# Causal attention: another order of the query blocks, two merged band steps, and other engines at the attentions' ends

## The chip, the cores and the metric

The kernel runs on one core of a Trainium2 chip. The metric is the device time of one execution, in microseconds (us), given as a median of several. Engines are named as in the profile: PE is TensorE's matrix multiplication (PEld its weight loads), DVE is VectorE, ACT is ScalarE, POOL is GpSimd and SP is SyncE, which here issues DMAs. Everything is computed in 32-bit floating point.

## The reference

The program is a block of two layers on an input of 2 sequences of 2048 tokens with 256 features. Every sublayer normalizes its input first and adds its result to it:

```python
x = x + 0.5 * _L0_ffn_ref(_layernorm(x), ...)   # mixture of 6 experts, two for each token
x = x + _L0_attn_ref(_layernorm(x), ...)        # full softmax attention, 16 heads of 16
x = x + 0.5 * _L0_ffn_ref(_layernorm(x), ...)
x = x + 0.5 * _L1_ffn_ref(_layernorm(x), ...)   # a gated recurrence over the 2 sequences
x = x + _L1_attn_ref(_layernorm(x), ...)        # causal attention
x = x + 0.5 * _L1_ffn_ref(_layernorm(x), ...)
```

The change is mostly in the causal attention:

```python
q = _apply_rotary_interleave(q, cos, sin); k = _apply_rotary_interleave(k, cos, sin)
q = q / sqrt(DIM_PER_HEAD)
scores = jnp.einsum('bhqd,bhkd->bhqk', q, k)
rel_idx = jnp.clip(pos[None, :] - pos[:, None], -32, 32) + 32
rel = rel_emb[rel_idx]
scores = scores + jnp.einsum('bhqd,qkd->bhqk', q, rel)
scores = jnp.where(causal[None, None], scores, NEG_INF)
attn = jax.nn.softmax(scores, axis=-1)
ctx = jnp.einsum('bhqk,bhkd->bhqd', attn, v)
ctx = ctx + jnp.einsum('bhqk,qkd->bhqd', attn, rel)
out = ctx.transpose(0, 2, 1, 3).reshape(B, L, MODEL_DIM) @ w_o.T
```

A key more than 32 places behind its query gets the same relative term as all such keys. So only a band of keys near each query needs a term of its own.

## The kernel before, in words

**Order.** Each engine runs its instructions in the order in which the program emits them; nothing reorders them. Loops over numbered steps write that order. A step's own work is found in tables, and other work ("jobs" and "sends") is put down for a step by number.

**Tiles.** A sequence has 4 blocks of 512 tokens; a block has four chunks of 128. The 16 heads form 4 groups of 4 heads (`J`). A unit of attention is a *group*: (sequence b, query block qc, head group g), 64 of them in the full attention and 32 in the causal one. For a group the kernel does two passes over the scores. The first finds each query's maximum: PE multiplies 128 queries by up to 512 keys for one head, and DVE reduces the product to a column of maxima. The second computes scores again with keys on the partitions, with the maximum subtracted, ACT takes exponentials, and PE multiplies by the values. An additional column of ones in the values gives the softmax's sum.

**attention1 (lines 1008 to 1420), the causal attention.** `groups` lists the 32 groups in the order of work. For a group of block qc the maxima pass has 4 qc + 3 *pieces* (`pieces`): first qc times four far pieces (one chunk of queries by a block of keys, L1149 with the reduction L1158), then three band pieces (chunks 0 and 1 together, chunk 2, chunk 3). A band is 160 keys wide for 128 queries. It is first loaded with the relative terms (`by_position` makes them, ACT writes them to DRAM, `band_load` on SP reads them back skewed), DVE adds scores and takes maxima in one instruction (L1179), then reduces all maxima of a chunk to their negative, `mneg` (L1192), and one step later POOL adds that to the chunk's band (L552, 128x640). The exponentials pass has as many pieces (`key_blocks`), one or two blocks of 128 keys each: PE transposes band pieces (L1260, L1266), multiplies the rest (L1250, L1243), and ACT takes exponentials, four 128x512 or 128x384 in a piece (L1274). The step after, `weighted` multiplies by the values (L1283).

**Steps.** The lists `Ms`, `Me`, `Es`, `Ee` give each group's first and last step of the two passes. A step does one exponentials piece and one maxima piece if it has both (a *paired* step), or only the one kind. A group's exponentials come after its maxima, and a group's band tile is one of three, so its maxima wait for an earlier group's exponentials. With the order of groups that is used before, there are 319 steps, of which 257 are paired, 31 look only for maxima and 31 take only exponentials. The first steps, below zero, are preparation alone.

**Jobs.** `queries`, `keys` and `vals` prepare a pair of groups or a block: PE multiplies by weights, ACT copies, DVE shuffles, and `rotate` does the rotary rotation with three 128x512 operations, on DVE at the negative steps (L1050 is the last of them) and on POOL at the others, one, two and three steps later (`later`, by way of the helper's line L552). `queries_out` and `keys_out` have ACT put rows of heads in place (L141). `subtract` brings maxima into the queries; `positions_load`, `positions_exp`, `positions_T` and `positions` turn the stored band into the sum over relative values; `divide` transposes a group's sum (L668) and divides (L671, L672); `outputs_T` and `outputs` multiply by the output weights (L682, L691) and add to x (L697). `ln_stats` and `ln_transpose` prepare the next block's normalization.

**gather (L651).** The result of every `weighted` and `positions` is in PSUM. ACT copies it (L654), and a step later POOL adds the copy to the group's sum (L552). Both attentions use it.

**The end.** After the causal attention the last sublayer, a recurrence over 8 blocks (number = 4 x sequence + block), begins. attention1's `tail` holds statistics, normalization and transposition of the blocks 0 and 4 (`n5.stats`, `n5.normal`, `n5.turn`), done under the last exponentials. `recurrence` normalizes the others itself (L99 to L127), and skips what is there. It calls `turn(0, 0)`, then `gate(0, ...)`, `normal(0, 1)` and, inside its loop, `turn(0, 1)`, where (0, 1) is block 4.

The profile's L-numbers are of this program:

Of the kernel before, what the change touches and what calls it, by code (L numbers as in the profile page):

```python
# [17 lines left out]
P = 128  # L18
# [14 lines left out]
G = 4  # L33
# [9 lines left out]
def macaron_kernel(ctx: ExitStack, tc: tile.TileContext, t: dict, out: bass.AP):  # L43
# [510 lines left out]
    class Pieces:  # L554
# [15 lines left out]
        def later(self, units, fn, *args):  # L570

            self.due.at(self.unit + units, fn, *args)
# [78 lines left out]
        def gather(self, t, pv, parts, q0=0):  # L651

            part = self.wk.tile([P, TB], F32, name="part", bufs=parts + 2)
            nc.scalar.copy(part[:, q0:], pv[:, q0:])  # L654
            if t not in self.o:
                self.o[t] = part
                return
            o = self.o[t][:, q0:]
            self.later(1, nc.gpsimd.tensor_tensor, o, o, part[:, q0:], ALU.add)
# [57 lines left out]
    def attention0(norm, tail, rest, wq, wk_, wv, wo, bff):  # L717
# [7 lines left out]
        with ExitStack() as s:  # L725
# [61 lines left out]
            def weighted(t, kb):  # L787
                b, qc, g = groups[t]
                pv = bank()
                for j in range(J):  # L790
                    h = (g % 2) * J + j
                    nc.tensor.matmul(  # L792
                        pv[rows(j), :], lhsT=v[b, g // 2][:, kb, ds(h * VW, 32)],
                        rhs=z.pTs.pop((t, kb, j)), start=True, stop=True,
                    )
                z.gather(t, pv, 4)
# [211 lines left out]
    def attention1(norm, tail, w, relk, relv, kbias, dramp, skew):  # L1008
# [4 lines left out]
        with ExitStack() as s:  # L1013
# [3 lines left out]
            for b in range(B):  # L1017
                groups += [(b, 1, g) for g in range(G)]
                for g in range(0, G, 2):
                    groups += [(b, qc, g + i) for qc in (2, 0) for i in range(2)]  # L1020
                groups += [(b, 3, g) for g in range(G)]
# [16 lines left out]
            def rotate(xa, wa, b, qc, g):  # L1038
# [8 lines left out]
                if z.unit < 0:  # L1047
                    nc.vector.tensor_tensor(xa, xa, cos[b, qc], ALU.mult)
                    nc.vector.tensor_tensor(xb, xb, sin[b, qc], ALU.mult)
                    nc.vector.tensor_tensor(xa, xa, xb, ALU.add)  # L1050
                else:
                    op = nc.gpsimd.tensor_tensor
                    z.later(1, op, xa, xa, cos[b, qc], ALU.mult)
                    z.later(2, op, xb, xb, sin[b, qc], ALU.mult)
                    z.later(3, op, xa, xa, xb, ALU.add)
# [3 lines left out]
            def keys(b, qc, g, own):  # L1059
# [9 lines left out]
                rotate(packed[b, qc, g], w["k"], b, qc, g)  # L1069
# [22 lines left out]
            def queries(t):  # L1092
# [5 lines left out]
                rotate(q[t + 1], w["q"], b, qc, g)  # L1098
# [45 lines left out]
            def largest(t, qbs, c, j):  # L1144
# [30 lines left out]
                for qb in qbs:  # L1175
# [12 lines left out]
                    done[t, qb] = done.get((t, qb), 0) + 1  # L1188
                    if done[t, qb] < J:
                        continue  # L1190
                    mneg = z.mnegs[t % 2][:, qb]
                    nc.vector.tensor_reduce(  # L1192
                        mneg[:, :, z.row(t)], mx[t][:, qb, :, 0 : qc + 1 + (qb > 0)], AX.X,
                        ALU.max, negate=True,
                    )
                    z.later(
                        1, nc.gpsimd.tensor_tensor, band[t][:, qb], band[t][:, qb],
                        mneg[:, :, ds(z.row(t), 1)].to_broadcast([P, J, BW]), ALU.add,
                    )
# [76 lines left out]
            def weighted(t, kbs):  # L1276
# [12 lines left out]
                z.gather(t, pv, 3, max(0, kbs[0] - qc * CPB) * P)  # L1289
# [70 lines left out]
            for b in range(B):  # L1360
                for qc in range(SB):
                    f = Ms[index[b, max(qc, 1), 0]]

                    done_ = {2: 1, 3: 0}.get(qc)
# [13 lines left out]
                    for half in range(2):  # L1378
                        due = Es[index[b, max(qc, 1), 2 * half]] - 2 + 2 * (qc == 0)
                        at(due if b or qc > 1 or half else -4, vals, b, qc, half)  # L1380
# [98 lines left out]
    with tc.manual_schedule(engines=ENGINES):  # L1479
# [71 lines left out]
        tail = []  # L1551
        for i, b in enumerate((0, SB)):
            tail += [(3 + 2 * i, n5.stats, b), (4 + 2 * i, n5.normal, b, nc.vector),
                     (5 + 2 * i, n5.turn, b)]
# [96 lines left out]
```

## Time and profile before

| | |
|---|---|
| median of 5 runs | 4017.53 us (4013.49 to 4020.42) |
| profiled execution: time, span | 4018.74 us, 4017.0 us |
| granted TensorE clock, mean | 0.994 |
| PE busy | 3969.3 us (99%), 29,024 instructions |
| DVE busy | 2699.1 us (67%), 6131 |
| ACT busy | 2555.0 us (64%), 5067 |
| POOL busy | 1620.5 us (40%), 1421 |
| causal attention, first score matmul of its first paired step to that of its last step | 2605.3 to 3820.9 us |
| last recurrence's first matmul | 3835.4 us |

The profiled execution is 1.2 us over the median. Its span is the recorded part; 1.7 us lie around it. In a line of groups or of a timeline, `L1192` is the source line, `out<-in` names tiles, then come shapes and counts, busy time and the mean of one in ns, and the idle time of that engine just before, with what ended it. "PE busy" is a modelled time: matmuls are pipelined, and PE counts as busy while it runs at another engine's pace, so a stretch is judged by looking at which engine is full beside it.

### The profile page before, as it was taken

The page shows a single profiled execution, that of the slowest core. Times are in us where ns is not written, and L with a number is a line of the kernel's source. Part 1 is how long each engine was busy: PE and PEld are TensorE (multiplying, and loading weights), DVE is VectorE, ACT ScalarE, POOL GpSimd, SP SyncE. Part 2 cuts the span into 40 slices and gives each one's busy share as a digit, 9 for nine tenths or more (in the row PEclk, how much of TensorE's full clock was granted, in tenths as well). Part 3 has the DMA queues.
Part 4 walks back from the last instruction along what each step waited for, and adds up shares of the span by engine and source line. Part 5 has one row for each costly group of instructions (what it writes and reads, how often), then busy time and mean ns, then how long its engine had stood idle before and what let it go on. Part 6 is the DMA issues. An engine that isn't in the chain of part 4 may idle for free.

```text
span 4017.0 us, 78045 instructions
## 1 busy us (share of the span) xinstructions
PE 3969.3 (99%) x29024; PEld 1957.9 (49%) x29024; DVE 2699.1 (67%) x6131; ACT 2555.0 (64%) x5067; POOL 1620.5 (40%) x1421
## 2 busy tenths in 40 slices
PE   8999999999999999999999999999999999999999
PEld 5665333333344333333345655555555555555445
DVE  6247888888877788888743344667777756667634
ACT  2333888888887888888853332366657776666832
POOL 5245333337333333333444331245536655453510
PEclk9999999999999999999999999999999999999999
DMA  7341000100000000000023420254442334543201
GB/s 267 119 129 56 1 1 1 48 1 2 1 1 1 1 1 1 1 1 2 10 95 129 130 82 11 57 102 99 98 95 56 86 74 93 111 83 64 68 1 42
DMA packets 355515, 223.28 MB, mean 56 GB/s; under 512 B 146625, under 2 KB 338497, under 8 KB 355137
## 3 DMA queue, kind: packets, MB, share of 16 engines
q1 hardware_dynamic: 276800, 176.33, 17.3%
q0 software_dynamic: 12288, 33.57, 2.6%
q10 hardware_dynamic: 66048, 8.39, 1.5%
q8 instruction: 231, 3.78, 0.4%
q14 instruction: 148, 1.20, 0.1%
HBM read 113.12 MB, written 105.12 MB: 54 GB/s over the span
## 4 chain that ended last, share of the span: by engine, by line
PE 92%; DVE 4%; ACT 2%; POOL 1%; issue 1%; DMA 0%; ACTq 0%; SPq 0%; DVEq 0%; POOLq 0%
PE s L780 14%; PE s L792 13%; PE s L766 11%; PE s L148 7%; PE s L1149 7%; PE s L1283 7%; PE s L394 6%; PE s L1250 6%; PE s L414 3%; PE s L157 2%; PE s L1260 2%; PE s L691 2%; PE s L1243 1%; PE s L1266 1%; PE s L614 1%; PE s L949 1%
## 5 line engine op out<-in xcount | busy, mean ns | idle before, releaser
L552 POOL TENSOR_TENSOR part<-part 128x512 f32<-128x512 f32 (+2 forms) x768 | 950.1, 1238 | 1394.6 <-ACT part L654 1390.6
L770 DVE TENSOR_REDUCE mx<-s 128x1 f32<-128x512 f32 x2048 | 1270.5, 682 | 295.5 <-PE s L766 295.1
L785 ACT ACTIVATE pT<-s 128x512 f32<-128x512 f32 x2048 | 1063.5, 617 | 199.0 <-PE s L766 195.5
L766 PE MATMUL s<-kT,q 32*128 32x512 f32 x4096 | 1027.6, 618 | 0.2 <-DVE mx L770 0.2
L780 PE MATMUL s<-q,kT 32*128 32x512 f32 x4096 | 1018.3, 616 | 1.0 <-DVE q L649 1.0
L1274 ACT ACTIVATE pT<-s 128x512 f32<-128x512 f32 (+1 forms) x1152 | 580.6, 584 | 207.7 <-PE s L1250 102.9
L780 PEld LDWEIGHTS s<-q,kT 32*128 32x128 f32 x4096 | 417.5, 184 | 460.2 <-DVE mx L770 376.5
L654 ACT COPY part<-s 128x512 f32<-128x512 f32 (+2 forms) x832 | 500.3, 602 | 164.2 <-PE s L792 57.7
L1158 DVE TENSOR_REDUCE mx<-s 128x1 f32<-128x512 f32 (+1 forms) x768 | 472.3, 678 | 154.3 <-PE s L1149 148.7
L792 PE MATMUL s<-pT,v 128*32 128x512 f32 x4096 | 549.2, 604 | 0.7 <-ACT pT L785 0.2
L766 PEld LDWEIGHTS s<-kT,q 32*128 32x128 f32 x4096 | 410.5, 184 | 136.6 <-ACT pT L785 78.3
L1149 PE MATMUL s<-kT,q 32*128 32x160 f32 (+6 forms) x2240 | 341.5, 429 | 0.0
L1283 PE MATMUL s<-pT,v 128*32 128x512 f32 (+3 forms) x2560 | 297.3, 539 | 5.0 <-ACT pT L1274 4.8
L394 PE MATMUL s<-we,xT 128*128 x592 | 278.7, 593 | 0.2 <-ACT xT L389 0.2
L1149 PE MATMUL s<-b,q 32*128 32x512 f32 (+7 forms) x1280 | 258.8, 512 | 1.9 <-DVE mx L1158 1.9
L792 PEld LDWEIGHTS s<-pT,v 128*32 128x32 f32 x4096 | 84.4, 108 | 351.0 <-ACT pT L785 327.6
L401 DVE TENSOR_TENSOR h<-sg,s 128x256 f32<-128x256 f32 x148 | 62.3, 421 | 286.2 <-ACT sg L399 286.2
L1250 PE MATMUL s<-q,kT 32*128 32x512 f32 (+3 forms) x1152 | 242.2, 508 | 0.0
L552 POOL TENSOR_TENSOR band<-band,mneg 128x640 f32<-128x640 f32 x128 | 160.1, 1262 | 155.6 <-DVE mneg L1192 86.1
L447 POOL DMA_INDIRECT yg<-results,at x128 | 124.7, 974 | 237.8 <-DMA results<-y 198.4
L1179 DVE CUSTOM_DVE_ANT_0 band<-s,band 128x160 f32<-128x160 f32 (+1 forms) x512 | 153.6, 314 | 96.2 <-PE s L1149 61.1
L1250 PE MATMUL s<-q,b 32*128 32x512 f32 (+3 forms) x896 | 212.0, 567 | 0.0
(227 smaller groups left out, 5158.7 us busy)
## 6 DMA issues: line engine op xcount, KB each, us to landing
band<-skew SPq DMA_DIRECT2D x32, 1280.0 KB, 6.3
pd<-band SPq DMA_DIRECT2D x32, 1280.0 KB, 9.3
xs<-places SPq DMA_DIRECT2D x148, 128.0 KB, 2.2
results<-y SPq DMA_DIRECT2D x148, 128.0 KB, 1.7
places<-zero SPq DMA_DIRECT2D x2, 4736.0 KB, 23.7
we<-in_we SPq DMA_DIRECT2D x12, 768.0 KB, 9.9
skew<-s ACTq DMA_DIRECT2D x32, 256.0 KB, 3.0
s<-pd SPq DMA_DIRECT2D x32, 256.0 KB, 4.5
```

Source lines behind the costliest of these rows:

```text
L394: nc.tensor.matmul(pu, lhsT=xT[n][:, ts(kc, P)], rhs=w[:, kc, ds(val[n], 2 * D)], start=kc == 0, stop=kc == 1,)
L552: fn(*args)
L654: nc.scalar.copy(part[:, q0:], pv[:, q0:])
L766: nc.tensor.matmul(ps, lhsT=q[t][rows(j), ts(qb, P)], rhs=kT[b, g][rows(j), ts(kc, TB)], start=True, stop=True,)
L770: nc.vector.tensor_reduce(mx[t][:, qb * J + j, kc : kc + 1], ps, AX.X, ALU.max)
L780: nc.tensor.matmul(st, lhsT=kT[b, g][rows(j), ts(kb, P)], rhs=q[t][rows(j), :], start=True, stop=True,)
L785: nc.scalar.activation(z.pTs[t, kb, j], st, AF.Exp)
L792: nc.tensor.matmul(pv[rows(j), :], lhsT=v[b, g // 2][:, kb, ds(h * VW, 32)], rhs=z.pTs.pop((t, kb, j)), start=True, stop=True,)
L1149: nc.tensor.matmul(ps[:, ds(cols, n)], lhsT=q[t][rows(j), ts(qb, P)], rhs=kT[b, c, g][rows(j), ds(k0, n)], start=True, stop=True,)
L1250: nc.tensor.matmul(ps[:, q0:], lhsT=k, rhs=q[t][rows(j), q0:], start=True, stop=True, skip_group_check=True,)
L1274: nc.scalar.activation(z.pTs[t, kbs, j][:, q0:], ps[:, q0:], AF.Exp)
L1283: nc.tensor.matmul(pv[rows(j), q0:], lhsT=v[b, kb // CPB, g // 2][:, kb % CPB, ds(h * VW, 32)], rhs=pT[:, ds(c0, TB - q0)], start=kb == kb ...
```

## The change

1. The order of a sequence's groups. Before: block 1 for all four head groups; then for each pair of head groups blocks 2 and 0; then block 3 for all. After: block 1, then block 2 for all; then for each pair blocks 3 and 0. The schedule has 315 steps then: 261 paired, 27 with maxima only, 27 with exponentials only. The tables of cosines and sines of a block take the place of another block's (`done_`).
2. `gather` gets an argument `last`: the last `weighted` of either attention is added by DVE straight from PSUM, in place of ACT's copy and POOL's addition.
3. `rotate` is told by its caller whether it goes to DVE (`first`): the queries of group 0 and the keys at negative steps do; the queries of groups 2 and 3, at a negative step, go to POOL. `later` with zero steps runs at once.
4. The chunks 0 and 1 get one reduction to `mneg` and one POOL addition (128x1280) together; the maxima column that chunk 0 does not have is set by a memset, one for each group.
5. Two `vals` of the first sequence's block 0 and block 1 go from step -4 to the steps 4 and 2.
6. `tail` holds block 0 alone; block 4's normalization is left to the recurrence.

By engine, ACT has 2 copies less; DVE 32 reductions and one addition less and 32 memsets more; POOL 31 additions less. Matmuls and transfers are equal in number.

```diff
@@ -569,7 +569,10 @@
 
         def later(self, units, fn, *args):
 
-            self.due.at(self.unit + units, fn, *args)
+            if units:
+                self.due.at(self.unit + units, fn, *args)
+            else:
+                fn(*args)
 
         def begin(self, unit):
             self.unit = unit
@@ -648,8 +651,14 @@
                 )
             nc.vector.tensor_tensor(self.q[t], self.q[t], pm, ALU.add)
 
-        def gather(self, t, pv, parts, q0=0):
-
+        def gather(self, t, pv, parts, q0=0, last=False):
+
+
+            if last:
+                nc.vector.tensor_tensor(
+                    self.o[t][:, q0:], self.o[t][:, q0:], pv[:, q0:], ALU.add
+                )
+                return
             part = self.wk.tile([P, TB], F32, name="part", bufs=parts + 2)
             nc.scalar.copy(part[:, q0:], pv[:, q0:])
             if t not in self.o:
@@ -793,7 +802,7 @@
                         pv[rows(j), :], lhsT=v[b, g // 2][:, kb, ds(h * VW, 32)],
                         rhs=z.pTs.pop((t, kb, j)), start=True, stop=True,
                     )
-                z.gather(t, pv, 4)
+                z.gather(t, pv, 4, last=(t, kb) == (NG - 1, NKB - 1))
 
             jobs = Jobs()
             at = jobs.at
@@ -1015,10 +1024,9 @@
             wk, q = z.wk, z.q
             groups = []
             for b in range(B):
-                groups += [(b, 1, g) for g in range(G)]
+                groups += [(b, qc, g) for qc in (1, 2) for g in range(G)]
                 for g in range(0, G, 2):
-                    groups += [(b, qc, g + i) for qc in (2, 0) for i in range(2)]
-                groups += [(b, 3, g) for g in range(G)]
+                    groups += [(b, qc, g + i) for qc in (3, 0) for i in range(2)]
             NG = len(groups)
             kT, v, mx, band, cos, sin, wb, st, pd, lead = ({} for _ in range(10))
             MX = SB + 1
@@ -1035,7 +1043,7 @@
                     d[b, qc] = wk.tile([P, TB], F32, name=n)
                     nc.sync.dma_start(out=d[b, qc], in_=t[n][:, ts(qc, TB)])
 
-            def rotate(xa, wa, b, qc, g):
+            def rotate(xa, wa, b, qc, g, first):
 
 
                 pa = bank()
@@ -1044,15 +1052,12 @@
                 xb = wk.tile([P, TB], F32, name="s2", bufs=4)
                 nc.vector.stream_shuffle(xb, xa, [i ^ 1 for i in range(32)])
 
-                if z.unit < 0:
-                    nc.vector.tensor_tensor(xa, xa, cos[b, qc], ALU.mult)
-                    nc.vector.tensor_tensor(xb, xb, sin[b, qc], ALU.mult)
-                    nc.vector.tensor_tensor(xa, xa, xb, ALU.add)
-                else:
-                    op = nc.gpsimd.tensor_tensor
-                    z.later(1, op, xa, xa, cos[b, qc], ALU.mult)
-                    z.later(2, op, xb, xb, sin[b, qc], ALU.mult)
-                    z.later(3, op, xa, xa, xb, ALU.add)
+
+                op = (nc.vector if first else nc.gpsimd).tensor_tensor
+                wait = z.unit >= 0
+                z.later(1 * wait, op, xa, xa, cos[b, qc], ALU.mult)
+                z.later(2 * wait, op, xb, xb, sin[b, qc], ALU.mult)
+                z.later(3 * wait, op, xa, xa, xb, ALU.add)
 
             packed = {}
 
@@ -1066,7 +1071,7 @@
                     packed[b, qc, g] = wk.tile([P, TB], F32, name="s2", bufs=4)
                 else:
                     packed[b, qc, g] = keys_tile(b, qc, g + 1)
-                rotate(packed[b, qc, g], w["k"], b, qc, g)
+                rotate(packed[b, qc, g], w["k"], b, qc, g, z.unit < 0)
 
             def keys_tile(b, qc, g):
                 if (b, qc, g) not in kT:
@@ -1095,7 +1100,7 @@
                 for i in range(2):
                     q[t + 1 - i] = wk.tile([P, TB], F32, name="q", bufs=6)
                     mx[t + i] = wk.tile([P, CPB, J, MX], F32, name="mx", bufs=2)
-                rotate(q[t + 1], w["q"], b, qc, g)
+                rotate(q[t + 1], w["q"], b, qc, g, t == 0)
 
             def queries_out(t):
                 for i in range(2):
@@ -1185,18 +1190,21 @@
                         nc.vector.tensor_reduce(
                             m[:, qc + 1 : qc + 2], ps[:, ds(at_ + BW, n)], AX.X, ALU.max
                         )
-                    done[t, qb] = done.get((t, qb), 0) + 1
-                    if done[t, qb] < J:
-                        continue
-                    mneg = z.mnegs[t % 2][:, qb]
-                    nc.vector.tensor_reduce(
-                        mneg[:, :, z.row(t)], mx[t][:, qb, :, 0 : qc + 1 + (qb > 0)], AX.X,
-                        ALU.max, negate=True,
-                    )
-                    z.later(
-                        1, nc.gpsimd.tensor_tensor, band[t][:, qb], band[t][:, qb],
-                        mneg[:, :, ds(z.row(t), 1)].to_broadcast([P, J, BW]), ALU.add,
-                    )
+                done[t, qbs] = done.get((t, qbs), 0) + 1
+                if done[t, qbs] < J:
+                    return
+                k = slice(qbs[0], qbs[-1] + 1)
+                mneg = z.mnegs[t % 2][:, k]
+                if qbs[0] == 0:
+                    nc.vector.memset(mx[t][:, 0, :, qc + 1], 3.0 * MASKED)
+                nc.vector.tensor_reduce(
+                    mneg[:, :, :, z.row(t)], mx[t][:, k, :, 0 : qc + 2], AX.X, ALU.max,
+                    negate=True,
+                )
+                z.later(
+                    1, nc.gpsimd.tensor_tensor, band[t][:, k], band[t][:, k],
+                    mneg[:, :, :, ds(z.row(t), 1)].to_broadcast([P, len(qbs), J, BW]), ALU.add,
+                )
 
             def band_store(t):
 
@@ -1286,7 +1294,8 @@
                             rhs=pT[:, ds(c0, TB - q0)], start=kb == kbs[0],
                             stop=kb == kbs[-1], skip_group_check=len(kbs) > 1,
                         )
-                z.gather(t, pv, 3, max(0, kbs[0] - qc * CPB) * P)
+                last = (t, kbs) == (NG - 1, key_blocks(qc)[-1])
+                z.gather(t, pv, 3, max(0, kbs[0] - qc * CPB) * P, last)
 
             def positions_load(t):
                 wb[t] = wk.tile([P, CPB, J * BAND], F32, name="s2", bufs=4)
@@ -1361,7 +1370,7 @@
                 for qc in range(SB):
                     f = Ms[index[b, max(qc, 1), 0]]
 
-                    done_ = {2: 1, 3: 0}.get(qc)
+                    done_ = {2: 1, 3: 2}.get(qc)
                     free = early[index[b, done_, G - 2]] + 4 if done_ is not None else f - 28
                     at(max(f - 28, free), tables, b, qc)
                     if b or qc > 1:
@@ -1377,7 +1386,7 @@
                         sends.at(max(out_, free), keys_out, b, qc, g)
                     for half in range(2):
                         due = Es[index[b, max(qc, 1), 2 * half]] - 2 + 2 * (qc == 0)
-                        at(due if b or qc > 1 or half else -4, vals, b, qc, half)
+                        at(due if b or qc > 1 or half else 4 - 2 * qc, vals, b, qc, half)
             for n, (b, qc, g) in enumerate(groups):
                 e = early[n - n % 2]
                 by = max(By[n], e + (6 if e < 0 else 8))
@@ -1548,10 +1557,7 @@
                     n4.xn.pop(cb - 2)
 
             recurrence(rec, n3, False, rest, normals, turns)
-        tail = []
-        for i, b in enumerate((0, SB)):
-            tail += [(3 + 2 * i, n5.stats, b), (4 + 2 * i, n5.normal, b, nc.vector),
-                     (5 + 2 * i, n5.turn, b)]
+        tail = [(1, n5.stats, 0), (2, n5.normal, 0, nc.vector), (3, n5.turn, 0)]
         attention1(n4, tail, a, relk, relv, kbias, dramp, skew)
         w1.close()
         with ExitStack() as s:
```

## The prediction

> **What bounds the kernel now.** The page comes first: busy time by engine, and the chain of work that ended last.
>
> ```profile
> span 4017.0 us, 78045 instructions
> PE 3969.3 (99%) x29024; PEld 1957.9 (49%) x29024; DVE 2699.1 (67%) x6131; ACT 2555.0 (64%) x5067; POOL 1620.5 (40%) x1421
> ...
> PE 92%; DVE 4%; ACT 2%; POOL 1%; issue 1%; DMA 0%; ACTq 0%; SPq 0%; DVEq 0%; POOLq 0%
> ```
>
> TensorE is busy 99% and carries 92% of the chain; the change leaves its 29,024 matmuls as they are. Only three things can move: time in which PE waits, time in which it is "busy" at another engine's pace, and time at half clock. So I went to the windows view of attention1 (2573 to 3835 us). Columns: window, its length, busy us and count of PE, PEld, DVE, ACT, POOL, granted clock, DMA share, GB/s.
>
> ```profile
> 2573.00:2605.00 32.00, 27.19 (x174) 14.41 (x171) 29.60 (x92) 8.99 (x17) 18.45 (x16) 0.84 0.36 90
> 2725.10:2737.10 12.00, 12.00 (x108) 6.35 (x108) 11.71 (x39) 1.41 (x5) 10.06 (x9) 1.00 0.33 66
> 2852.50:2860.50 8.00, 8.00 (x72) 4.37 (x69) 7.89 (x19) 3.77 (x9) 2.95 (x3) 1.00 0.48 105
> 2973.90:2994.70 20.80, 20.09 (x151) 14.23 (x151) 19.22 (x66) 4.11 (x10) 9.41 (x8) 0.92 0.27 53
> ...
> 3599.30:3620.10 20.80, 20.09 (x151) 13.61 (x151) 18.07 (x65) 3.76 (x8) 9.41 (x8) 0.92 0.17 39
> 3670.20:3725.90 55.70, 55.70 (x526) 27.78 (x522) 42.49 (x113) 42.60 (x84) 24.97 (x21) 1.00 0.28 58
> 3779.30:3821.90 42.60, 42.60 (x362) 16.43 (x358) 13.57 (x33) 41.31 (x87) 23.90 (x22) 1.00 0.37 90
> ```
>
> Row 1 is the start, rows 2 to 5 are stretches of steps that only look for maxima: DVE is busy 92 to 99%, so PE's full bar is DVE's pace. Row 6 is paired steps (maxima of one group, exponentials of another): DVE 76%, ACT 76%, PE bounds. Row 7 is the exponentials-only end: ACT 97%. Last, the timeline where the attentions end and the recurrence begins (start, us, engine, line, operation; in brackets the idle time before it and its releaser):
>
> ```profile
> 2040.67 2.60 POOL L552 TENSOR_TENSOR part<-part 128x512 f32<-128x512 f32 x2 [1.18 <-ACT part L654]
> 2043.32 0.66 PE L668 MATMUL s<-ident,part 128*128 128x128 f32 x4 [2.18 <-POOL part L552]
> ...
> 3828.01 0.66 PE L668 MATMUL s<-ident,part 128*128 128x128 f32 x4 [2.18 <-POOL part L552]
> 3829.48 1.08 PE L682 MATMUL s<-ident,b 128*128 128x128 f32 x4 [0.37 <-DVE b L672]
> 3830.35 5.01 PE L691 MATMUL s<-a_o,b 128*128 128x256 f32 x16
> ...
> 3841.88 1.38 DVE L117 TENSOR_SCALAR b<-x,mv,rstd 128x256 f32<-128x256 f32 x4 [1.48 <-POOL rstd L106]
> ```
>
> Each attention ends in a 2.18 us wait of PE for ACT's copy and POOL's addition. The sixteen output matmuls behind it take 5.01 us, because the clock is halved for one window of about 3.4 us.
>
> To price stretches I cut the trace at each step's first score matmul. Against each kind of step's own undisturbed pace (the quarter-best of its kind; 2.93 us for a plain paired step), the steps from 2605.3 to 3820.9 us (1215.6 us) hold some 42 us of excess: maxima-only stretches with the few steps that catch up behind them 3.0, 2.5, 5.8 in batch 0 and 2.4, 2.5, 5.8 in batch 1 (22.0); exponentials-only stretches inside 3.9; the steps that prepare batch 1 6.7; the exponentials-only end 4.1; the rest spread thin.
>
> **The change, part by part.**
>
> **1. Order of the groups: maxima-only stretches.** After the start, the schedule has 22 maxima-only steps in six stretches (4, 2, 6 in each batch order); changed, 18 in five (4, 4, 2, 4, 4), since the six-step stretches ahead of the last query block go. At the excess of like stretches (4 steps 3.0, 2 steps 2.5, 6 steps 5.8; I price the new ones 4.2, 3.5, 2.5, 4.2, 3.5, as two of them now hold a normalization's statistics, 4 x 0.60 us of DVE each) 22.0 becomes 17.9: **-4.1**, from -9 (each at the 1 us of the best paired stretch) to 0.
>
> **2. Exponentials-only stretches inside.** Four of two steps (0.6 each) and one of six (1.5), 3.9, become one of six and one of four: 2.0, **-1.9** (-3 to +1).
>
> **3. Steps that prepare batch 1.** Key, value and normalization parts of batch 1 spread over steps of the fourth block, which have more far pieces: 6.7 to 4.5, **-2.2**. That size is a judgment between the 1.9 that the like steps of batch 1 show without preparing (-4.8) and 0.
>
> **4. attention1's end.** Seventeen exponentials-only steps stay. Before, 15 wide (4 x 0.610 us of ACT) and 2 narrow (4 x 0.494 us), 40.6 us; after, 12 and 5, 39.2: -1.4. Then the last chain. Before, 14.5 us from the last step's first matmul to the recurrence's (3820.9 to 3835.4), of which 8.0 is PE work: 6.5 waits, slow clock and ACT's pace. After, the last group is of the first query block; outputs of the fourth block (5 us) stand between, and the relative positions of groups 30 and 31 follow the weighted sums. The wait for copy and addition (2.18) stays, because `positions` is gathered by ACT and POOL; DVE's new direct addition there is no longer last. Waits 5.2, -1.3. Together **-2.7**, from -5 to +4 (another 2.18 for group 30, and another half-clock window of 1.7).
>
> **5. attention0's end.** One 0.69 us DVE addition instead of copy 0.59 and POOL 1.27. POOL's addition for the part before ends at about 2041.94 and binds DVE: transposes could start near 2042.75, not 2043.32. **-0.6** (-1.3 to 0).
>
> **6. attention1's start.** queries[2]'s rotation goes from DVE (3 x 0.69 = 2.07) to POOL (3 x 1.27 = 3.8). ACT's masked copies of those queries (1.48 us, queued behind it) come about 1.7 later, and with ACT's order the keys behind, 0.8 on the path. Two value additions (0.62 us each, DVE) move from before the start into steps 2 and 4, where DVE bounds (row 1). DVE's saving of 2.07 and the 0.8 and 1.24 nearly cancel; with 1.7 for POOL's length on the path, **+1.7** (-2 to +4).
>
> **7. Recurrence.** Only block 0's normalization is ready before it; block 4's now runs inside. The same chain for a later block, statistics to the end of the normalization, takes 5.1 us (3838.18 to 3843.26); behind DVE's state update (3851.46) its transposes are ready some 2.3 us after PE comes to them (3854.2). Transposes 0.9 (they leave part 4's cover, where ACT bounds), wait 2.3, half of a half-clock window's 1.7 loss: **+4.1** (+1 to +6).
>
> On that last half window: a single wait of 2.18 and 0.37 us was followed by a clock of 0.51 from 3829.5 to 3833.0. The Trainium skill (TensorE: Matmul & The Clock Gate, "HAM oscillation — how this bites in real kernels") says the clock falls for PE gaps longer than about 3.4 us; by it a 2.3 us wait costs nothing more and part 7 would be 3.2. The trace contradicts it, with a shorter gap.
>
> **8. One maximum and one addition for two bands.** DVE: 32 of 128 L1192 maxima (0.168 us) go, 32 memsets (0.165) come. POOL: 64 additions of 128x640 (1.262) become 32 of 128x1280 (about 2.5). **0**: POOL is 40% busy, the addition comes a step after the maximum and its band is transposed three steps later. If that cover goes, half a group's addition, 1.26 us, shows in each of 32 groups: +40 at worst.
>
> **9. Transfers.** Band stores, band loads and the load of the relative positions move with their groups; SP issues the same 32 of each, in the same order within a group and at the same distances in steps (load 6 ahead of its maxima, store 3 behind). The load takes 6.3 us and the store 9.3 from issue to landing against steps of 2.9: **0** as now (0 to +6, one band late once, where maxima-only steps run faster).
>
> Sum: -4.1 - 1.9 - 2.2 - 2.7 - 0.6 + 1.7 + 4.1 = **-5.7**, on the profiled execution's 4018.7 (span 4017.0 and 1.7 around it): 4013.0. That execution lies 1.2 above the median of the runs, so the median forecast is about 4012.
>
> **Rivals.** *The DVE-bound stretches give nearly all back.* If parts 1 to 3 go to their lower ends (-9, -3, -4.8) and the rest stays, the sum is -14 and the time 4003. For: rows 2 to 5 show DVE at its limit. Against: 18 such steps stay. *The new end and the recurrence cost more (other side).* Group 31's positions chain cannot start before its band is stored, loaded back (4.5 us to landing) and put through ACT; if no work covers that load, PE stands some 6 us and falls to half clock once more (+8 on part 4; with part 7 at +6, sum +4), and if group 30's chain waits in turn (+4), the time is 4026. For: the load of group 31 is issued only after the last exponentials. Against: weighted sums and outputs of 7 us lie between. It decides from 14 us of added wait. *Merged addition late*: from a third of the groups on (11 x 1.26 = 14) also slower. *Nothing happens*: PE is 99% busy and every gain is given back in the next paired stretch, as PE bounds there: 4017.
>
> **How the numbers follow.** Within 0.2% (8 us) of 4017.5 is what this measurement can hardly tell from no change: 4009.5 to 4025.6. Forecast (sum between 0 and -9) 0.45, of which 0.08 lies past -8; full gain 0.28; nothing 0.10; the slower rivals 0.12, half of it the end; what I have not seen 0.05, put to slower. Faster: 0.28 + 0.08 = 0.36; slower 0.12 + 0.05 = 0.17; same 0.47. The range runs from the full gain with a late start gained too (3999) to the rival's 4026 and a little (4029).
>
> **What would show it.** Parts 1 and 2: the DVE-bound windows of 20.8 us ahead of the last block gone, none longer than 4 steps. 4: after the last exponential, 20 to 24 us to the recurrence with PE idle 3 or less. 5: the wait before attention0's last L668 group 1.5 to 1.7. 6: first paired step later by 1 to 2 us after the start. 7: one wait of 2 to 3 us before the transposes of block 4. 8: no PE wait for POOL's band. I am wrong if the paired stretches themselves, 2.93 us a step, move by 0.02 us or more (300 steps: 6 us), or if PE waits for a DMA anywhere.

## The result and the profile after

The changed kernel takes 4024.8 us (median of 21, 4022.88 to 4029.18), the kernel before 4016.3 (median of 41): a ratio of 1.0022, 95% interval 1.0016 to 1.0028. It is 8.5 us slower, where 5.7 us faster was forecast. The changed kernel's profiled execution took 4024.1 us, with a span of 4022.4.

Its page begins like the one before. In the chain, the share of no engine changes:

```profile
span 4022.4 us, 77958 instructions
PE 3968.3 (99%) x29024; PEld 1946.3 (48%) x29024; DVE 2693.0 (67%) x6130; ACT 2553.5 (63%) x5065; POOL 1615.8 (40%) x1390
...
PE 92%; DVE 4%; ACT 2%; POOL 1%; issue 1%; DMA 0%; ACTq 0%; SPq 0%; DVEq 0%; POOLq 0%
```

So the time has to be looked for in windows. Every four-step maxima-only stretch of the changed order (columns as in the prediction):

```profile
2724.00:2737.90 13.90, 13.27 (x108) 6.68 (x108) 13.54 (x43) 1.41 (x5) 6.91 (x6) 1.00 0.46 71
2914.60:2928.40 13.80, 12.14 (x97) 6.24 (x97) 11.65 (x38) 3.40 (x7) 8.80 (x7) 0.88 0.40 78
3352.60:3368.10 15.50, 14.87 (x107) 6.84 (x107) 13.95 (x44) 1.14 (x3) 7.74 (x6) 0.89 0.51 77
3544.80:3558.80 14.00, 12.34 (x97) 6.11 (x97) 11.63 (x38) 3.10 (x5) 8.85 (x7) 0.88 0.40 76
```

The first and third are the steps 37 to 40 and 191 to 194, the others 85 to 88 and 239 to 242. The same four steps 37 to 40 took 12.0 us before. Three of the four lose clock (0.88, 0.89), and in the second and fourth DVE is *not* full: 11.6 of 14 us. PE stands for 1.7 us there.

The timeline of the second stretch shows why:

```profile
2914.56 0.95 PE L1154 MATMUL s<-kT,q 32*128 32x160 f32 x16
...
2915.51 0.33 DVE L1184 CUSTOM_DVE_ANT_0 band<-s,band 128x160 f32<-128x160 f32 x1 [1.48 <-PE s L1154]
...
2916.44 1.17 PE L1154 MATMUL s<-kT,q 32*128 32x160 f32 x16
...
2917.41 1.55 PE L1154 MATMUL s<-b,q 32*128 32x512 f32 x8
...
2917.97 0.31 DVE L1184 CUSTOM_DVE_ANT_0 band<-s,band 128x160 f32<-128x160 f32 x1
...
2918.88 0.55 PE L648 MATMUL s<-ident,mneg 128*128 128x128 f32 x3
...
2920.86 0.18 DVE L1200 TENSOR_REDUCE mneg<-mx 128x4 f32<-128x20 f32 x1
...
2921.09 0.33 PE L648 MATMUL s<-ident,mneg 128*128 128x128 f32 x1 [1.66 <-DVE mneg L1200]
...
2923.69 2.46 PE L157 MATMUL s<-b,a_q 128*32 128x512 f32 x16
...
2926.08 2.05 PE L617 MATMUL s<-a_v,b 128*128 128x128 f32 x16
```

The stretch begins with two band pieces. PE needs 0.95 and 1.17 us for their products; DVE needs about 2.5 and 3 us for their additions, maxima and reductions (from 2915.51 to 2917.97, and from there to 2921.04). PE runs ahead, through the next products, to `subtract` (L648), which transposes the last chunk's maxima. They are there only at 2921.0. PE waits 1.66 us, and only afterwards comes to work that does not need that maximum: the queries (L157) and the values (L617). The windows view around that wait shows the clock that was granted: 0.74 on average in 2919 to 2924.

```profile
2919.00:2924.00 5.00, 3.34 (x16) 1.37 (x20) 4.89 (x14) 0.00 (x0) 3.73 (x4) 0.74 0.06 21
```

In the steps 37 to 40 of the kernel before, the queries stand ahead of the transposes (there L645), and these don't wait:

```profile
2726.75 1.17 PE L1149 MATMUL s<-kT,q 32*128 32x160 f32 x16
2727.84 1.92 PE L157 MATMUL s<-b,a_q 128*32 128x512 f32 x16
...
2731.36 0.66 PE L645 MATMUL s<-ident,mneg 128*128 128x128 f32 x4
```

The groups view adds up PE's idle time ahead of `subtract`, in the kernel before and then in the changed one. The part that the causal attention's own `mneg` (L1192, now L1200) ended goes from 1.4 to 4.6 us; the rest is the full attention's:

```profile
L645 PE MATMUL s<-ident,mneg 128*128 128x128 f32 x256 | 42.7, 287 | 3.0 <-DVE mneg L773 1.6 <-DVE mneg L1192 1.4
```

```profile
L648 PE MATMUL s<-ident,mneg 128*128 128x128 f32 x256 | 43.1, 288 | 6.2 <-DVE mneg L1200 4.6 <-DVE mneg L782 1.6
```

Attention0's end went as written, and the recurrence nearly so. In the timeline the wait before `divide` is 1.56 us in place of 2.18, and block 4's transposes wait 1.25 us for their normalization:

```profile
2040.87 0.69 DVE L658 TENSOR_TENSOR part<-part,s 128x512 f32<-128x512 f32 x1 [12.34 <-POOL part L552]
2041.62 0.66 PE L677 MATMUL s<-ident,part 128*128 128x128 f32 x4 [1.56 <-DVE part L658]
...
3858.14 1.64 PE L127 MATMUL s<-ident,b 128*128 128x128 f32 x8 [1.25 <-DVE b L117]
```

Between the marks of the two profiled executions (us):

| from, to | before | after | difference |
|---|---|---|---|
| start to attention1's first query product | 2559.7 | 2555.8 | -3.9 |
| to the first paired step | 45.6 | 48.4 | +2.8 |
| to the last exponentials step | 1215.6 | 1210.5 | -5.1 |
| to the recurrence's first product | 14.3 | 21.3 | +7.0 |
| to the end | 181.8 | 186.4 | +4.6 |

Of the first row 0.6 is the change's; the other 3.3 lie in code that the change leaves alone, where this execution met fewer half-clock windows. Without them the difference is 8.7, close to the 8.5 of the medians.

### The profile page after: what moved, and what is told of

The parts are those of the page before. It is cut to its first block, busy times and chain, and to the rows that moved or that the text cites. A ratio compares the mean times of both kernels' runs of the same rounds, so it can differ in the third digit from the quotient of the medians.

```text
span 4022.4 us, 77958 instructions
## 1 busy us (share of the span) xinstructions
PE 3968.3 (99%) x29024; PEld 1946.3 (48%) x29024; DVE 2693.0 (67%) x6130; ACT 2553.5 (63%) x5065; POOL 1615.8 (40%) x1390
## 4 chain that ended last, share of the span: by engine, by line
PE 92%; DVE 4%; ACT 2%; POOL 1%; issue 1%; DMA 0%; ACTq 0%; SPq 0%; DVEq 0%; POOLq 0%
PE s L789 14%; PE s L801 13%; PE s L775 11%; PE s L1154 7%; PE s L148 7%; PE s L1291 7%; PE s L394 6%; PE s L1258 6%; PE s L414 3%; PE s L157 3%; PE s L1268 2%; PE s L700 1%; PE s L1251 1%; PE s L1274 1%; PE s L617 1%; PE s L958 1%
## 5 line engine op out<-in xcount | busy, mean ns | idle before, releaser
L552 POOL TENSOR_TENSOR part<-part 128x512 f32<-128x512 f32 (+1 forms) x766 | 948.1, 1238 | 1410.4 <-ACT part L663 1407.8
L552 POOL TENSOR_TENSOR band<-band,mneg 128x640 f32<-128x640 f32 (+1 forms) x96 | 155.8, 1622 | 138.5 <-DVE mneg L1200 109.6
```

Of the source, the lines that this page charges most:

```text
L552: fn(*args)
```

## The experiments

Theory 1 from here on: the order costs, by the stretches and by block 4's normalization. Theory 2: the order gains what was forecast, and the merged maximum and addition cost more. Theory 3: only the end costs.

**The order alone.** The kernel before with

```diff
-                groups += [(b, 1, g) for g in range(G)]
+                groups += [(b, qc, g) for qc in (1, 2) for g in range(G)]
                 for g in range(0, G, 2):
-                    groups += [(b, qc, g + i) for qc in (2, 0) for i in range(2)]
-                groups += [(b, 3, g) for g in range(G)]
+                    groups += [(b, qc, g + i) for qc in (3, 0) for i in range(2)]
...
+        tail = [(1, n5.stats, 0), (2, n5.normal, 0, nc.vector), (3, n5.turn, 0)]
```

and the tables' places as in the change.

> The kernel before with the new order of groups alone, and what hangs on it: the tables' places and the tail without block 4. Theory 1 (the order itself costs: the maxima-only stretches are fewer but each leaves PE more often at DVE's pace, and block 4's normalization moves into the recurrence): +6.4 us on before, of which +1.8 up to the recurrence and +4.6 in it. Theory 2 (the order gains what was forecast, and the merged maximum and addition delay the bands): -7 to 0. Theory 3 (only the end costs): +4.6, with the steps from 9 on unchanged in sum.

Measured: 4025.3 us against 4015.5, ratio 1.0027 (1.0015 to 1.0038). The order, with the tail that hangs on it, brings the whole loss; theory 2 falls.

**Everything but the order.** The changed kernel with those lines as before.

> The changed kernel with the order of groups, tail and tables of before: only the ends on other engines, the merged maximum and addition, the rotation on POOL and the later values remain. Theory 1: +2.2 us on before (start +2.8, attention0's end -0.6). Theory 2: +8 to +15, and PE or ACT waiting for POOL's band additions. Theory 3: +2 to +4.

Measured: 4013.9, ratio 0.9999 (0.9990 to 1.0008). Cut into the same steps, its excess over a clean pace equals that of before to 0.2 us in every segment but the two six-step stretches (4.2 each and not 5.8, one half-clock window less). So the merged maximum and addition cost nothing that can be seen. The start is longer by 2.9 (48.5 us), and the end shorter by 1.9 (12.5 us from the last exponentials step to the recurrence): there the last weighted sum is the path, and DVE's direct addition replaces the copy and POOL. Of the 1.9, 0.6 is the wait (1.56 us and not 2.18) and 1.3 the half-clock window that did not follow it. In two of the four kernels with this end such a window came a little later, in the recurrence (183.4 and 183.5 us in place of 181.8), so only the 0.6 is sure.

**The order in the first sequence only.** The end is as before.

```diff
+                if b == 0:
+                    groups += [(b, qc, g) for qc in (1, 2) for g in range(G)]
+                    for g in range(0, G, 2):
+                        groups += [(b, qc, g + i) for qc in (3, 0) for i in range(2)]
+                    continue
```

> The changed kernel with the new order in the first sequence only; the second sequence, the tail and so the end are as before. Theory 1: the first sequence's stretches and the start, +2.2 + 2.2 = +4.4 us on before. Theory 2: +8 or more. Theory 3 (end and recurrence carry the loss): about +2, that is only the start and attention0's end.

Measured: 4020.4, ratio 1.0013 (1.0004 to 1.0022), +4.9 us. The rest of the change, which this kernel also has, measured 0.9999 by itself, so about half the loss comes with the first sequence's order, and theory 3 is not enough.

**The start as before.** Rotation of queries[2] on DVE, values at step -4.

```diff
-                rotate(q[t + 1], w["q"], b, qc, g, t == 0)
+                rotate(q[t + 1], w["q"], b, qc, g, z.unit < 0)
...
-                        at(due if b or qc > 1 or half else 4 - 2 * qc, vals, b, qc, half)
+                        at(due if b or qc > 1 or half else -4, vals, b, qc, half)
```

> The changed kernel with the start of before: the rotation of the second pair of queries on DVE, all values of the first blocks at step -4 or as before. If the start's +2.8 us comes from these two moves: 2.8 us under the changed kernel, +5.7 on before, and the stretch from the first key product of attention1 to its first paired step 45.6 us long again and not 48.4. If it is the clock windows' place that made it longer: no difference to the changed kernel.

Measured: 4021.7, ratio 1.0017 (1.0008 to 1.0026), some 3 us under the changed kernel, an interval wide enough to hold 0 to 6. The start itself took 46.7 us, 1.8 under the changed kernel and 1.1 over the one before. So in these profiles about 2 us are these moves', and 1 is not explained by them. In five later profiles with the changed start it took 49.8 to 50.0 us at a lower clock (0.83 from 2557.7 to 2607.7 in the changed kernel's repeat, 0.86 in the result's profile, 0.89 before): one half-clock window more, and the moves then cost some 3.

The next four runs were on a chip on which the kernel before takes 4147.4 us; the experts' stages are longer there, the segments of attention1 agree with those of the other chips to 0.1 us. Times are therefore given as ratios.

**Less work for DVE in the stretches**, in either kernel (the maxima of those pieces are left incomplete):

```diff
-                        mx[t][:, qb, j, c : c + 1], ps[:, 0:n], AX.X, ALU.max
+                        mx[t][:, qb, j, c : c + 1],
+                        ps[:, 0 : n if z.unit < 9 or z.unit in exp_at else 64], AX.X, ALU.max
```

> The kernel before, in which far pieces in steps that only look for maxima (from step 9 on) reduce 64 of their columns and not all 512; the maxima are so left incomplete there, everything else is computed. 14 steps, 56 reductions, each some 0.5 us shorter on DVE. If DVE's pace is what the maxima-only stretches cost (20.4 us over their clean pace with the steps behind them): 8 to 14 us faster than before. If the stretches wait for something else (a chain through mneg, a band's transfer, the clock): 0 to 4.

> The same for the changed kernel: 10 steps, 40 reductions. If DVE's pace is the cost (23.7 us in five stretches): 6 to 12 us under the changed kernel, that is -3 to +3 on before, and less gained than by the same edit of the kernel before, since half of its maxima-only steps are band pieces, which stay. If the stretches wait for something else: 0 to 4 under the changed kernel.

Measured: 0.9989 (0.9980 to 0.9998) and 1.0018 (1.0009 to 1.0027): 4.5 us and, against the changed kernel's 1.0022, about 2, which the intervals can't tell from nothing. Less than DVE's pace would give. The windows view of the steps 69 and 70, in the kernel before and then with short reductions:

```profile
2852.47:2860.51 8.04, 8.04 (x73) 4.41 (x70) 7.92 (x19) 3.79 (x9) 2.95 (x3) 1.00 0.48 105
```

```profile
2986.44:2994.12 7.68, 7.68 (x72) 4.11 (x69) 4.46 (x19) 3.80 (x9) 3.17 (x4) 1.00 0.45 106
```

DVE loses 3.5 of its 7.9 us, and the window 0.36. DVE's 99% there was no bound: PE had 7.7 us of its own work. The other stretches of the kernel before also shorten by 0.4 to 0.5 us, the four steps 37 to 40 from 12.0 to 11.5; only the two six-step ones lose 2.1 (20.8 and 20.9 to 18.8), and 1.6 of that is a half-clock window that each of them no longer has. That takes away the reading on which the prediction's first part stood. Theory 4 took its place: what costs is PE coming to a wait for the last maximum with its own work still behind that wait. Theory 5 is the old one, that the sum of DVE's work sets a stretch's length.

**Block 4's normalization left out** (the recurrence takes block 0's for it):

```diff
+                if (cb, step) == (0, 1) and store:
+                    norm.xnT[SB] = norm.xnT[0]
+                    return
```

> The changed kernel in which the last recurrence takes block 0's transposed normalization for block 4 also, so that block 4's statistics, normalization and transposition are left out. If these cost on the path what the profiles show between the recurrence's start and its end (185.2 against 182.3 us, and 0.9 of transposes that left attention1's end): 3 to 4.6 us under the changed kernel. If they are hidden and the difference is the clock's: 0 to 1.

Measured: 1.0014 (1.0005 to 1.0023), about 3 us under the changed kernel's ratio, though that lies inside the interval; the trace is clearer. The recurrence takes 181.8 us, as it did before the change; with block 4's normalization it took 184.6 to 184.7 in four of the profiles with the new end, and 186.3 to 186.4 in the others, the result's among them. So this part costs 2.9, or 4.6 where a half-clock window falls in. In the profiles without that window in the recurrence it lay just ahead of it: the stretch from the last exponentials step to the recurrence was then longer, 22.2 to 22.6 us and not 21.3.

**The changed kernel again, values two steps ahead, and subtract a step later**, on one chip:

> The changed kernel without an edit, so that the next two are compared with it on the same chip. Both theories: 8 to 10 us on before (ratio 1.0022), and PE's idle time before the subtract transposes that is put to attention1's mneg 4.6 us, against 1.4 in the kernel before.

Measured: 4024.9, ratio 1.0023 (1.0014 to 1.0033).

```diff
+            for unit in sorted(jobs):
+                lone = [u > 8 and u in largest_at and u not in exp_at for u in (unit - 2, unit)]
+                if all(lone):
+                    moved = [j for j in jobs[unit] if j[0] is vals]
+                    jobs[unit] = [j for j in jobs[unit] if j[0] is not vals]
+                    jobs[unit - 2] = moved + jobs.get(unit - 2, [])
```

> The changed kernel, with the value products that stand in the last step of a four-step maxima-only stretch done two steps earlier, ahead of subtract (steps 40, 88, 194, 242 to 38, 86, 192, 240). Theory 4 (in these stretches two steps of band pieces take DVE some 3 us each and PE 1, so PE comes to subtract before the last maximum, waits, and the clock halves): PE has 1.9 us of work there, the waits of 0.6 to 1.7 go and with them most of the half-clock windows: 5 to 10 us under the changed kernel, and the 4.6 us before subtract fall to about 1. Theory 5 (the stretch's sum of DVE work sets its length): 0 to 1, since DVE has as much to do.

Measured: 4016.7, ratio 1.0003 (0.9994 to 1.0012): **8.2 us under the changed kernel**, from four value products that were moved two steps. The windows of the four stretches, in the changed kernel on this chip and with the values ahead:

```profile
2727.51:2743.05 15.54, 14.91 (x108) 6.86 (x108) 13.98 (x44) 1.45 (x5) 7.78 (x6) 0.89 0.52 89
2919.75:2933.75 14.00, 12.34 (x98) 6.13 (x98) 11.66 (x38) 3.40 (x7) 8.84 (x7) 0.88 0.40 90
3357.92:3371.81 13.89, 13.26 (x107) 6.68 (x107) 13.50 (x43) 1.15 (x3) 6.90 (x6) 1.00 0.43 76
3548.51:3562.51 14.00, 12.34 (x97) 6.13 (x97) 11.65 (x38) 3.10 (x5) 8.84 (x7) 0.88 0.40 86
```

```profile
2725.42:2738.12 12.70, 12.55 (x107) 6.51 (x107) 12.31 (x40) 1.45 (x5) 6.71 (x5) 1.00 0.38 73
2914.83:2925.95 11.12, 11.12 (x98) 5.78 (x97) 9.96 (x34) 3.13 (x7) 8.11 (x6) 1.00 0.21 59
3350.47:3363.18 12.71, 12.56 (x108) 6.51 (x108) 12.32 (x40) 1.15 (x3) 6.71 (x5) 1.00 0.38 74
3539.87:3550.99 11.12, 11.12 (x97) 5.78 (x97) 9.96 (x34) 2.87 (x5) 8.10 (x6) 1.00 0.20 58
```

Together 57.4 us become 47.7, and the clock is whole. DVE and PE do the same work; only its order has changed (DVE's addition of the values, L625, moves with them, and 1.2 to 1.7 us of DVE's work in each stretch now falls behind the window). The steps behind pay little for it, 0.3 us each behind the second and fourth stretch: from the first paired step to the last exponentials step the profiles take 1210.7 and 1201.6 us. Theory 5, the sum of DVE's work, falls. The second and fourth stretch say it most clearly, as DVE is at 90% there and PE full; in the first and third DVE stays at 97%. In the second stretch's timeline the values now stand ahead of `subtract`, which no longer waits:

```profile
2916.70 1.17 PE L1154 MATMUL s<-kT,q 32*128 32x160 f32 x16
...
2917.80 2.05 PE L617 MATMUL s<-a_v,b 128*128 128x128 f32 x16
...
2920.85 0.83 PE L648 MATMUL s<-ident,mneg 128*128 128x128 f32 x4
```

The other way to take that wait away:

```diff
-                jobs.at(Me[n] + 1, z.subtract, n)
+                late = Me[n] + 1 in largest_at and Me[n] + 1 not in exp_at and Me[n] > 8
+                jobs.at(Me[n] + 1 + late, z.subtract, n)
```

> The changed kernel, with subtract a step later where the step after a group's last maxima has maxima only, so that PE has the next step's products ahead of it. Theory 4: 4 to 9 us under the changed kernel, if the exponentials behind don't wait for the subtracted queries in turn (the group's first exponentials come one step after; then 0 to 3). Theory 5: 0.

Measured: 4022.3, ratio 1.0019 (1.0010 to 1.0028), 2.6 us under the changed kernel, with intervals that overlap, not the 4 to 9. The exponentials behind were not late: the paired steps took as long as without the edit, to 0.1 us. Its timeline in the fourth stretch shows what was late next. The wait for `mneg` is gone, but the products that PE now does instead need free space in PSUM, which DVE, behind with the band pieces (L1190), gives back one at a time:

```profile
3552.94 4.53 PE L1154 MATMUL s<-b,q 32*128 32x512 f32 x16
...
3554.32 0.29 PEld L1154 LDWEIGHTS s<-b,q 32*128 32x128 f32 x2 [0.66 <-DVE mx L1190]
3554.99 0.29 PEld L1154 LDWEIGHTS s<-b,q 32*128 32x128 f32 x2 [0.38 <-DVE mx L1190]
...
3557.39 0.76 PE L648 MATMUL s<-ident,mneg 128*128 128x128 f32 x4
```

Sixteen such products take 4.53 us here. And though PE shows no wait in this stretch, the clock fell all the same, to 0.88 on average:

```profile
3548.00:3562.00 14.00, 14.00 (x92) 5.32 (x91) 12.13 (x47) 4.22 (x8) 9.16 (x7) 0.88 0.23 58
```

So it isn't enough that PE has something ahead of `subtract`; it has to be work that does not wait for DVE itself. This sharpens theory 4, which had not distinguished the two.

**A version that beats both.** The order, tail and start of before, the ends by DVE, the merged maximum and addition, and the copy of `positions_T` on ACT in steps without exponentials:

```diff
-                nc.vector.tensor_copy(wb[t].rearrange("p a d -> p (a d)"), pw)
+                copy = nc.vector.tensor_copy if z.unit in exp_at else nc.scalar.copy
+                copy(wb[t].rearrange("p a d -> p (a d)"), pw)
```

> The order, tail and start of before, the ends by DVE and the merged maximum and addition of the change, and one edit of my own: the copy in positions_T goes to ACT where a step has no exponentials (6 copies of 0.69 us leave DVE in the maxima-only stretches). If DVE's pace bounds there: 2 to 4 us from these, 0.6 + 1.5 from the ends, in all 3 to 6 us faster than before. If not: the ends' 1 to 2 alone.

Measured: ratio 0.9987 (0.9978 to 0.9995), 5.4 us faster than before, inside the 3 to 6 that were expected if DVE's pace bounds. The traces agree in part: against "Everything but the order", which differs from this kernel by these copies and by the start, the steps 37 to 40 go from 12.0 to 11.4 us and the first six-step stretch from 19.25 to 18.5, nearly the whole 0.69 us of the copy that DVE no longer makes there, while the two-step stretches stay. So DVE's work does count where PE later waits for what stands behind it; it is the sum that doesn't. With the values of three stretches two steps ahead as well:

> The order, tail and start of before, both attentions' ends by DVE, the merged maximum and addition, the copy of positions_T on ACT in steps without exponentials, and value products two steps ahead as above (steps 40, 104, 258). Theory 4: 1 to 3 us under what the same without the moved values gave (ratio 0.9987), so 6 to 8 under before. Theory 5: no difference to that, 5 under before.

Measured: 4008.3 against 4015.8, ratio 0.9984 (0.9975 to 0.9993), **7.4 us faster than before**, 16.6 under the changed kernel. It ran on another chip than the version without the moved values, so what these add here (the two intervals overlap) is not shown by times. In its windows the steps 37 to 40 take 11.1 us and the six-step stretches 17.3 and 19.0, against 11.4, 18.5 and 20.2 without the moved values (12.0, 20.8 and 20.9 before). But the paired step behind each of them takes 3.7 us in place of 2.9, and in it PE and its weight loads wait for DVE's reductions (L1164; 0.2 and 0.4 us behind the first). Over all steps the two profiles differ by 0.6 us (1211.6 and 1211.0). In this order the moved values thus bring next to nothing that the traces show, and theory 4's 1 to 3 us is not shown here.

## Why the prediction was wrong

The outcome was on the side of the rival that was given 0.12, and was not that rival's mechanism.

- **Part 1 failed, in size, sign and cause.** It priced the new stretches at 4.2, 3.5, 2.5, 4.2, 3.5; they hold 4.2, 5.9, 1.6, 5.8, 6.1 us of excess. The sum goes from 22.0 to 23.6 and not to 17.9. The step that failed is the price by the number of steps, from stretches called like: the new four-step stretches took 13.8 to 15.5 us, and the one that they were priced by 12.0. That one was not like them: there PE had the queries' 1.9 us ahead of `subtract`, and the new order puts queries or keys, and values, behind it. Under it lay the reading that DVE at 92 to 99% bounds these stretches; the short reductions contradict it, and the moved values show what costs in the changed order. (The six stretches of before are of 4, 2, 6 and 2, 2, 6 steps, not 4, 2, 6 twice as the prediction has it; its sum of 22 steps and its prices are of the right ones.)
- **Parts 2 and 3 failed too.** Forecast at -4.1, the steps between the stretches gained 5.2 us of excess (13.0 to 18.2). Where, is read from the trace alone and hangs on what is called a step's clean pace, since steps hold other work too. By the one used here it is the pairs of second blocks 3.1 to 7.2, the exponentials-only stretches and the preparation of sequence 2 8.2 to 8.8, the rest in the last paired steps. The raw time does not bear out the first of these: paired steps with both groups of block 2 take 4.30 us each before (46 steps) and 4.07 after (62), and a plain paired step stays at 2.93. So which paired steps lose, and why, stays open; no run tried it.
- **Part 4 was about right,** by the same clean pace. The recurrence's first product comes 7.0 us later after the last exponentials step, or 8.2 in the repeat; 11.4 of clean work left the steps before, and the exponentials-only end lost 0.5. With the 0.9 of transposes that part 7 counts, this is -4.0 and -2.8, against -2.7. Its bound names a second wait for POOL, for group 30, and that came: 1.65 us, then 2.07 for group 31. Between the marks, without any clean pace, the parts 1 to 4 together gave +1.9 (-5.1 in the steps, +7.0 behind them) where -10.9 was forecast; how that splits is an estimate.
- **Part 5 was right**: -0.6 (a wait of 1.56 and not 2.18).
- **Part 6** was forecast at +1.7, and measured +2.8, inside its bounds; in the profiles with one half-clock window more it was +4.2 to +4.4, just past them.
- **Part 7** was right in kind, 4.1 against 4.6 in that profile and 2.9 elsewhere. The wait was 1.25 and not 2.3, and a whole half-clock window fell in where half of one was counted, so the nearness to 4.6 is in part luck.
- **Parts 8 and 9 were right**: the merged addition took 2.34 us, and no matrix multiplication waited for it or for a transfer of a band.

With these the marks give 1.6 + 5.2 - 4.0 - 0.6 + 2.8 + 4.6 and, for the transposes that moved, -0.9: 8.7 us. Parts 1 to 3 are off by 15 us, all the others together by less than 1. Of the 15, by the clean pace used here, 5.7 are part 1's, whose cause the moved values show; 9.3 are parts 2 and 3's, whose cause is open.

The prediction weighed a rule of the Trainium skill (TensorE: Matmul & The Clock Gate, "HAM oscillation — how this bites in real kernels"): avoid gaps of PE of over about 3.4 us. Read as "a shorter one costs nothing", it does not hold here: these runs too show the clock at half after a single wait of 1.66 us. The prediction saw this at the attentions' ends and should have applied it to part 1 as well: a stretch in which PE waited 1.7 us lost another 1.7 to the clock.

## What to carry to other kernels

In a window where one engine is 99% busy and the other's busy time is modelled, ask what PE still has to do of its own: here 3.5 us less work on the 99% engine shortened such a window by 0.36. Price a stretch by what stands ahead of its first wait, not by its number of steps, and put work that needs neither the late result nor the late engine's buffers ahead of that wait: four value products moved by two steps were worth 8.2 us in the changed order. Then look at the step behind: in the order of before the same move shortened three stretches by 2.7 us together and lengthened the step behind each by 0.8. A change of order that leaves the matrix multiplications as they were can lose more by such waits than it gains in fewer unpaired steps.

## What the runs showed of the hardware

- A half-clock window of some 3.4 us (1.7 us lost) followed waits of PE far shorter than itself. In the four stretches with the values behind, three had a mean clock of 0.88 to 0.89; with the values ahead all four had 1.00. It came after both waits of 1.66 us, and after only one of the two of 0.63 us: in the result's profile after the third stretch's, in the repeat after the first's. In the kernel with subtract a step later it came (mean clock 0.88) without any recorded wait, after sixteen products at DVE's pace in 4.53 us. So a wait is not the only thing that brings it.
- One POOL addition of 128x1280 took 2.34 us, two of 128x640 2 x 1.26: merging them saves 0.18, no more.
- Stretches of unpaired steps in attention1 repeated to 0.1 us from run to run, and from chip to chip, but for whole half-clock windows of 1.6 to 1.7 us. Differences of single parts can thus be read from one profile each, where the medians' intervals of some 3.5 us cannot tell them.
